# A mixture-of-experts stage: the inner features made turned, for three slots of tokens at once

## The chip, the cores and the metric

The program runs on one core of a Trainium2 chip. The metric is the device time of one execution in microseconds (us); lower is better. The kernel before takes 1195.88 us (median of three runs, 1195.74 to 1195.96).

The engines are named as in the profile: PE is TensorE (matrix multiply), PEld its weight loads, DVE is VectorE, ACT is ScalarE, POOL is GpSimd, SP is SyncE. Each works through its own queue in order.

## The reference

One block of a graph transformer on 1250 nodes with 768 features: a layer norm, a two-layer graph attention and a linear attention added to the input, and then a feed-forward layer with eight experts. The change concerns that last part alone:

```python
def _L0_ffn_ref(x, Wg, bg, W1, b1, W2, b2):      # DIM 768, 8 experts, HIDDEN 384, TOP_K 2
    gate = xt @ Wg + bg
    scores, idx = jax.lax.top_k(gate, TOP_K)
    h = jax.nn.gelu(jnp.einsum('td,edh->eth', xt, W1) + b1[:, None, :], approximate=False)
    y = jnp.einsum('eth,ehd->etd', h, W2) + b2[:, None, :]
    comb = jnp.sum(jax.nn.one_hot(idx, NUM_EXPERTS, dtype=x.dtype) * scores[..., None], axis=1)
    out = jnp.einsum('te,etd->td', comb, y)
...
x = x + _L0_ffn_ref(_layernorm(x, axis=-1)[None], ...)[0]
```

Every node goes to its two best experts, weighted with the raw scores. All is in float32.

## The kernel before

The program first builds the graph attention (up to line 581), then the linear attention (to 648), then, tile by tile of 125 nodes, queries, the sum of the branches, the second layer norm and the routing (lines 767 to 895). The normalised rows are written to a table in DRAM, `xl_d`; the sum so far goes to the output in DRAM. Routing leaves, for each expert, lists of node numbers in *slots* of 128 (`idx`) with the weights (`gs`).

The stage of the experts stands in lines 898 to 971. `slot` (line 904) computes one slot of 128 tokens for one expert:

1. an indirect DMA on POOL's queue gathers 128 rows of `xl_d` into `xg` (three buffers, line 908);
2. TensorE turns them in six transposes into `px` (two PSUM banks, one buffer, line 911), and two DVE copies bring them to `xsT` (line 915);
3. first layer: six matmuls with the tokens standing and 384 weight columns moving give `ph`, tokens on the partitions (line 919); DVE copies it to `h` (922), three more transposes turn it into `pt` (925), and three activations on ACT add the bias, now one number per partition, and apply the Gelu, into `hT` (928);
4. second layer: six matmuls with hT standing give `py` (two banks, one buffer, line 933);
5. DVE adds the bias (936), ACT multiplies by the gate weight (937) into `ys` (two buffers), and an indirect DMA on POOL's queue adds the 128 rows to the output in DRAM (938).

Each expert gets three slots in any case (`FIX`, lines 941 to 946). One further slot, of an expert that is only known at run time, is computed after that (`other(0)`, line 970), and more of them stand behind branches that are not taken here: the trace has 25 slots. Weights of an expert (2.3 MB, `expert`, line 653) lie in a ring of four buffers; the load for expert e + 4 is issued on SP's queue after expert e, and it needs the buffer that expert e's last matmul releases. The bias rows of the second layer have two buffers.

The order of instructions on each engine isn't the order of the text. A planner takes, by its own costs, the earliest instruction of the text that is ready when an engine is free; the engines then work through the order that results. Waits between engines, also the wait for a buffer and the wait of one scatter-add to the output for the one before it, are added automatically.

Of the kernel before, what the change touches and what calls it, by code (L numbers as in the profile page):

```python
# [27 lines left out]
F32 = mybir.dt.float32  # L28
# [5 lines left out]
AF = mybir.ActivationFunctionType  # L34
ALU = mybir.AluOpType
AX = mybir.AxisListType
PSUM = bass.MemoryType.PSUM

N, D = 1250, 768
PT, NT = 125, 10  # L40
KC = D // 128
H1, C1, H2, C2 = 4, 192, 2, 96
HEADS, DH = 12, 64
NE, FF = 8, 384
FC = FF // 128
# [8 lines left out]
NJ = -(-N // 128)  # L54
FIX = 3
# [14 lines left out]
def gps_block(ctx: ExitStack, tc: tile.TileContext, x, src, dst, norm_g, norm_b, W1, a_src1, a_dst1,  # L70
              b1, W2, a_src2, a_dst2, b2, Wu, bu, Wq, bq, Wk, bk, Wv, bv, Wo, bo, Wg, bg, fW1, fb1,
              fW2, fb2, out):
    nc = tc.nc
# [43 lines left out]
    ident = const.tile([128, 128], F32)  # L117
# [13 lines left out]
    xl_d = dram.tile([N + 128, D], F32)  # L131
# [40 lines left out]
    rows = fl.tile([KC, 128], F32)  # L172
# [67 lines left out]
    with tc.If(nc.values_load(odd[0:1, 0:1], min_val=0, max_val=1) > 0), ExitStack() as es:  # L240
# [9 lines left out]
        for j in range(NT):  # L250
# [21 lines left out]
            for g0 in range(0, NT, 4):  # L272
                n = min(4, NT - g0)
# [266 lines left out]
    with tc.tile_pool(name="wp", bufs=3) as wp, tc.tile_pool(name="rb", bufs=1) as rb:  # L540
        with tc.tile_pool(name="ag_p1", bufs=1, space=PSUM) as ag_p:
            for hd in range(H1):
# [10 lines left out]
                v = ag[:, :, :2 * CG].rearrange("p a (b c) -> p a b c", b=2)  # L553
# [44 lines left out]
    for t in range(NT):  # L598
# [3 lines left out]
        for k in range(2):  # L602
            half = slice(k * 384, (k + 1) * 384)
            for w in (Wk_sb, Wv_sb):
                ps = bank()
                for c in range(KC):
                    nc.tensor.matmul(ps[:PT, :384], xnT[:, c, t * PT:(t + 1) * PT], w[:, c, half],  # L607
                                     start=c == 0, stop=c == KC - 1)
# [11 lines left out]
            for c in range(3):  # L620
                nc.tensor.matmul(ps[:, c * 129:(c + 1) * 129],
                                 ky[:, (3 * k + c) * 128:(3 * k + c + 1) * 128], va[:, 3 * k + c],
                                 start=c == 0, stop=c == 2, skip_group_check=True)
# [29 lines left out]
    def expert(w1, w2, b2):  # L653

        t = wt.tile([128, KC, D], F32, name="w", bufs=4).rearrange("p c f -> p (c f)")
        nc.sync.dma_start(t[:, :KC * FF].rearrange("p (c f) -> p c f", c=KC),
                          w1.rearrange("(c p) f -> p c f", p=128))
        nc.sync.dma_start(t[:, KC * FF:].rearrange("p (c d) -> p c d", c=FC),
                          w2.rearrange("(c p) d -> p c d", p=128))
        b = fp.tile([128, D], F32, name="wb", bufs=2)  # L660
        nc.sync.dma_start(b, row_bcast(b2, 128))
        return t, b
# [27 lines left out]
    ring = [expert(fW1[0], fW2[0], fb2[0])]  # L690
    outr = out[:N].rearrange("(t p) d -> p t d", p=PT)
    xlr = xl_d[:N].rearrange("(t p) d -> p t d", p=PT)
    idx = fp.tile([128, NV + 1], I32)
    gs = fp.tile([128, NV + 1], F32)
    fb1T = fp.tile([128, FC, NE], F32)
# [3 lines left out]
    with ExitStack() as rs:  # L699
# [68 lines left out]
        for t in range(NT):  # L768
# [10 lines left out]
            for i, (l, r) in enumerate(parts):  # L779
                for k in range(2):  # L780
                    nc.tensor.matmul(po[k][:, :384], l, r[:, k * 384:(k + 1) * 384],  # L781
                                     start=i == 0, stop=i == len(parts) - 1)
# [5 lines left out]
            for h in range(H2):  # L788
                for k in range(2):
# [3 lines left out]
                                     stop=True)  # L793
# [9 lines left out]
            xT = rl.tile([128, KC, PT], F32, name="xT")  # L803
            turn(xT, xl, u_p, "u", nc.scalar.copy)
            pg = g_p.tile([128, 2 * NV], F32, name="g")
            for c in range(KC):
                nc.tensor.matmul(pg[:PT, :NE], xT[:, c], Wg_sb[:, c], start=c == 0,
                                 stop=c == KC - 1)
# [38 lines left out]
            for k in range(2):  # L847
# [3 lines left out]
                for i, v in enumerate((node1[:, t:t + 1], both[:, 1, k:k + 1])):  # L851
# [4 lines left out]
                                 stop=k == 1 and t == NT - 1)  # L856
# [9 lines left out]
        pt = g_p.tile([128, 2 * NV], F32, name="g")  # L866
# [32 lines left out]
    sp = ctx.enter_context(tc.tile_pool(name="sp", bufs=2))  # L899
    x_p = ctx.enter_context(tc.tile_pool(name="x_p", bufs=1, space=PSUM))  # L900
    h_p = ctx.enter_context(tc.tile_pool(name="h_p", bufs=2, space=PSUM))
    y_p = ctx.enter_context(tc.tile_pool(name="y_p", bufs=1, space=PSUM))

    def slot(w, rows, gates, bias):

        w, wb = w
        xg = sp.tile([128, D], F32, name="xg", bufs=3)
        nc.gpsimd.indirect_dma_start(xg, None, xl_d, bass.IndirectOffsetOnAxis(rows, 0))
        px = x_p.tile([128, 2, 512], F32, name="px")
        for c in range(KC):  # L910
            nc.tensor.transpose(px[:, c // 3, (c % 3) * 128:(c % 3 + 1) * 128],  # L911
                                xg[:, c * 128:(c + 1) * 128], ident)
        xT = sp.tile([128, KC, 128], F32, name="xsT")
        for a in range(2):
            nc.vector.tensor_copy(xT[:, 3 * a:3 * a + 3],  # L915
                                  px[:, a, :384].rearrange("p (b n) -> p b n", b=3))
        ph = h_p.tile([128, FF], F32, name="ph")
        for c in range(KC):
            nc.tensor.matmul(ph, xT[:, c], w[:, c * FF:(c + 1) * FF], start=c == 0,  # L919
                             stop=c == KC - 1)  # L920
        h = sp.tile([128, FF], F32, name="h")
        nc.vector.tensor_copy(h, ph)
        pt = h_p.tile([128, FC, 128], F32, name="pt")
        for f in range(FC):
            nc.tensor.transpose(pt[:, f], h[:, f * 128:(f + 1) * 128], ident)
        hT = sp.tile([128, FC, 128], F32, name="hT")
        for f in range(FC):
            nc.scalar.activation(hT[:, f], pt[:, f], AF.Gelu, bias=bias[:, f])  # L928
        py = y_p.tile([128, 2, 512], F32, name="py")
        for f in range(FC):  # L930
            for k in range(2):
                o = KC * FF + f * D + k * 384
                nc.tensor.matmul(py[:, k, :384], hT[:, f], w[:, o:o + 384], start=f == 0,  # L933
                                 stop=f == FC - 1)
        ys = sp.tile([128, D], F32, name="ys")
        nc.vector.tensor_add(halves(ys), py[:, :, :384], halves(wb))  # L936
        nc.scalar.mul(ys, ys, gates)
        nc.gpsimd.indirect_dma_start(out, bass.IndirectOffsetOnAxis(rows, 0), ys, None,
                                     compute_op=ALU.add)

    for e in range(NE):
        for j in range(FIX):
            v = e * NJ + j
            slot(ring[e], idx[:, v:v + 1], gs[:, v:v + 1], fb1T[:, :, e:e + 1])
        if e + 4 < NE:
            ring.append(expert(fW1[e + 4], fW2[e + 4], fb2[e + 4]))

    def other(k):

        ve = nc.values_load(v_row[0:1, k:k + 1], min_val=0, max_val=NV,  # L950
                            engines=[mybir.EngineType.DVE])
        ee = nc.values_load(e_row[0:1, k:k + 1], min_val=0, max_val=NE - 1,
                            engines=[mybir.EngineType.DVE, mybir.EngineType.SP])
        rows = sp.tile([128, 1], I32, name="rows")
        nc.vector.tensor_copy(rows, idx[:, bass.ds(ve, 1)])
        gates = sp.tile([128, 1], F32, name="gates")
        nc.vector.tensor_copy(gates, gs[:, bass.ds(ve, 1)])
        bias = sp.tile([128, FC, 1], F32, name="bias")
        nc.vector.tensor_copy(bias, fb1T[:, :, bass.ds(ee, 1)])
        w = expert(fW1[bass.ds(ee, 1)].rearrange("o d f -> (o d) f"),  # L960
                   fW2[bass.ds(ee, 1)].rearrange("o d f -> (o d) f"), fb2[bass.ds(ee, 1)])
        slot(w, rows, gates, bias)

    def others(k):
        if k < MORE:
            with tc.If(nc.values_load(n_more[0:1, 0:1], min_val=0, max_val=MORE) > k):
                other(k)
                others(k + 1)

    other(0)  # L970
    others(1)

# [31 lines left out]
```

## Time and profile before

| | |
|---|---|
| median of three runs | 1195.88 us |
| the profiled execution | 1195.09 us |
| its span, first to last instruction | 1193.0 us |
| graph and linear attention, 0 to 610 us | PE busy 543.69 |
| queries and routing, 610 to 936 us | PE busy 314.82 |
| experts, 936 to 1181.2 us | PE busy 234.81 of 245.20 |
| from the last scatter-add's issue to the end | 11.8 us |

"Busy" is the time in which at least one instruction of the engine ran. A float32 matmul stands in the trace as two records, so a matmul written once in the text counts twice. PEclk is the share of TensorE's full clock that was granted. A row of a group gives busy time and mean duration in ns, then the idle time of the engine just before, and what ended it. The mean duration of a PE record includes its way through the array; how far two records stand apart is read from their starts.

### The profile page before, as it was taken

How to read it: one execution, taken by the hardware profiler on the slowest of the kernel's cores; microseconds unless marked ns; L12 is line 12 of the kernel's file. 1: busy time of each engine (PE TensorE's matmuls, PEld its weight loads, DVE VectorE, ACT ScalarE, POOL GpSimd, SP SyncE). 2: the span in 40 equal slices, each digit the busy share in tenths (PEclk: the TensorE clock that was granted, in tenths of full speed). 3: DMA queues.
4: the chain of work that ended last, by engine and by line, in shares of the span. 5: the costliest groups of instructions: out<-in, count | busy, mean ns of one | idle time of the engine just before them, and what ended most of it. 6: DMA issues, size and time to landing. Idle time of an engine off the chain costs nothing.

```text
span 1193.0 us, 12366 instructions
## 1 busy us (share of the span) xinstructions
PE 1093.3 (92%) x4634; PEld 729.2 (61%) x4634; DVE 683.0 (57%) x1391; ACT 365.2 (31%) x575; POOL 76.8 (6%) x100
## 2 busy tenths in 40 slices
PE   2599988999999999899989999999998699999994
PEld 1586656587878788545545666666665455555552
DVE  6866666779797876696723655555555322222221
ACT  2141115273827272455621211111110012121121
POOL 1000000000000000000000000000000122232221
PEclk9599999999999999999989999999999699999998
DMA  5014000000000001000090111111134357667432
GB/s 154 27 50 162 20 20 1 1 1 1 1 1 1 1 1 53 1 0 1 29 385 4 39 39 39 39 39 39 39 118 158 118 143 195 178 175 184 104 67 42
DMA packets 33282, 79.62 MB, mean 67 GB/s; under 512 B 5258, under 2 KB 13020, under 8 KB 33208
## 3 DMA queue, kind: packets, MB, share of 16 engines
q1 hardware_dynamic: 27608, 59.02, 15.0%
q0 software_dynamic: 5600, 19.66, 8.2%
q8 instruction: 40, 0.66, 0.2%
q14 instruction: 34, 0.28, 0.1%
HBM read 60.37 MB, written 18.30 MB: 66 GB/s over the span
## 4 chain that ended last, share of the span: by engine, by line
PE 70%; DVE 21%; DMA 4%; issue 2%; ACT 2%; POOL 1%; DVEq 0%; SPq 0%; POOLq 0%; ACTq 0%
PE po L781 13%; PE ph L919 9%; PE py L933 7%; PE mm L430 7%; PE mm L607 7%; PE mm L751 7%; DVE scr L515 6%; DVE w L535 5%; DVE w L536 5%; PE ag L548 3%; PE u L792 2%; PE ag L569 2%; PE mm L405 2%; DMA w<-in_L_gnn_Wu_dram 2%; PE px L911 1%
## 5 line engine op out<-in xcount | busy, mean ns | idle before, releaser
L548 PE MATMUL ag<-kept,w 125*125 125x198 f32 x800 | 137.4, 333 | 5.1 <-DVE w L536 4.9
L548 PEld LDWEIGHTS ag<-kept,w 125*125 125x125 f32 x800 | 133.5, 188 | 9.0 <-DVE w L536 9.0
L919 PE MATMUL ph<-w,xsT 128*128 128x384 f32 x300 | 110.1, 505 | 3.2 <-DVE xsT L915 0.7
L933 PE MATMUL py<-w,hT 128*128 128x384 f32 x300 | 101.0, 487 | 0.5 <-ACT hT L928 0.5
L430 PE MATMUL mm<-Wg,xnT 128*125 128x400 f32 x240 | 91.0, 517 | 1.0 <-DVE xnT L321 0.6
L607 PE MATMUL mm<-Wv_sb,xnT 128*125 128x384 f32 x240 | 85.7, 489 | 4.8 <-DVE kvacc L627 4.8
L535 DVE TENSOR_TENSOR w<-v,w 125x1250 f32<-125x1250 f32 x60 | 86.3, 1454 | 5.9 <-ACT w L533 5.2
L936 DVE TENSOR_TENSOR ys<-py,wb 128x768 f32<-128x768 f32 x25 | 23.9, 957 | 113.9 <-issue 98.3
L781 PE MATMUL po<-w,xnT 128*125 128x384 f32 x240 | 84.8, 496 | 3.1 <-DMA w<-in_L_gnn_Wu_dram 3.1
L515 DVE CUSTOM_DVE_ANT_0 scr<-ss_row,mask 125x1250 bf16<-125x1250 f32 x60 | 87.2, 1453 | 0.5 <-ACT ss_row L506 0.2
L536 DVE SCALAR_TENSOR_TENSOR w<-w,AT 125x1250 f32<-125x1250 f32 x60 | 86.4, 1455 | 0.4
L534 ACT ACTIVATE v<-dn_row,sl 125x1250 f32<-125x1250 f32 x60 | 79.3, 1333 | 17.3 <-DVE w L535 16.8
L607 PE MATMUL mm<-Wk_sb,xnT 128*125 128x384 f32 x240 | 84.4, 486 | 0.0
L751 PE MATMUL mm<-w,xnT 128*125 128x384 f32 x240 | 84.2, 489 | 0.0
L919 PEld LDWEIGHTS ph<-w,xsT 128*128 128x128 f32 x300 | 56.3, 194 | 43.8 <-DVE xsT L915 9.0
L933 PEld LDWEIGHTS py<-w,hT 128*128 128x128 f32 x300 | 56.8, 190 | 40.4 <-ACT hT L928 1.2
L781 PE MATMUL po<-w,qT 128*125 128x384 f32 x240 | 80.8, 486 | 0.0
L781 PEld LDWEIGHTS po<-w,xnT 128*125 128x125 f32 x240 | 44.2, 190 | 30.6 <-DMA w<-in_L_gnn_Wu_dram 3.3
L781 PEld LDWEIGHTS po<-w,qT 128*125 128x125 f32 x240 | 44.2, 188 | 29.4
L607 PEld LDWEIGHTS mm<-Wv_sb,xnT 128*125 128x125 f32 x240 | 42.4, 187 | 31.1 <-DVE kvacc L627 6.9
L751 PEld LDWEIGHTS mm<-w,xnT 128*125 128x125 f32 x240 | 43.6, 188 | 27.6 <-ACT qT L321 0.2
L430 PEld LDWEIGHTS mm<-Wg,xnT 128*125 128x125 f32 x240 | 43.2, 192 | 26.8 <-ACT v L367 1.4
(277 smaller groups left out, 1436.3 us busy)
## 6 DMA issues: line engine op xcount, KB each, us to landing
w<-in_L_ffn_W_dram SPq DMA_DIRECT2D x18, 1152.0 KB
xt<-in_x_dram SPq DMA_DIRECT2D x20, 336.0 KB
wb<-in_L_ffn_b_dram SPq DMA_DIRECT2D x9, 384.0 KB
out_dram<-xt SPq DMA_DIRECT2D x10, 336.0 KB
xl_d<-xl SPq DMA_DIRECT2D x10, 336.0 KB
W_sb<-in_L_gnn_W_dram SPq DMA_DIRECT2D x1, 2304.0 KB
Wk_sb<-in_L_mix_Wk_dram SPq DMA_DIRECT2D x1, 2304.0 KB
Wv_sb<-in_L_mix_Wv_dram SPq DMA_DIRECT2D x1, 2304.0 KB
```

The lines of the kernel that those rows point to most:

```text
L430: nc.tensor.matmul(ps[:PT, :2 * (CG + 2)], xnT[:, c, t * PT:(t + 1) * PT], Wg1[:, c, 2 * k:2 * k + 2].rearrange("p h c -> p (h c)"), start ...
L515: nc.vector.tensor_tensor_reduce(scr, ss_row, mask[:, t], 1.0, 0.0, ALU.mult, ALU.max, top[:, t:t + 1])
L534: nc.scalar.activation(v, dn_row, AF.Exp, bias=sl[:, st:st + 1])
L535: nc.vector.tensor_tensor(w, v, w, op=ALU.max)
L536: nc.vector.scalar_tensor_tensor(w, w, 2.0, AT[:, st, :N], op0=ALU.min, op1=ALU.mult)
L548: nc.tensor.matmul(ag[:, t // 2, o:o + CG], w[:, t * PT:(t + 1) * PT], gw[:, st, hd], start=st == 0 and t % 2 == 0, stop=st == NT - 1, ski ...
L607: nc.tensor.matmul(ps[:PT, :384], xnT[:, c, t * PT:(t + 1) * PT], w[:, c, half], start=c == 0, stop=c == KC - 1)
L751: nc.tensor.matmul(ps[:PT, :384], xnT[:, c, tk], Wq_sb[:, c, half], start=c == 0, stop=c == KC - 1)
L781: nc.tensor.matmul(po[k][:, :384], l, r[:, k * 384:(k + 1) * 384], start=i == 0, stop=i == len(parts) - 1)
L919: nc.tensor.matmul(ph, xT[:, c], w[:, c * FF:(c + 1) * FF], start=c == 0, stop=c == KC - 1)
L933: nc.tensor.matmul(py[:, k, :384], hT[:, f], w[:, o:o + 384], start=f == 0, stop=f == FC - 1)
L936: nc.vector.tensor_add(halves(ys), py[:, :, :384], halves(wb))
```

## The change

`slot` is split in three. `gather(rows)` fetches and turns the rows of up to three slots into one `xsT` of 384 columns. `hidden` makes the inner features already turned: the weights' 128 x 128 blocks stand, and the tokens' columns, 384 of them, move, so that the bias and Gelu go straight from `ph` to `hT`; the copy to `h` and the transposes to `pt` go. `give` is the second layer and the scatter-add for one slot, as before. The loop over experts calls `hidden` for an expert, then `gather` for the next one, then `give` three times. `py` gets two buffers, in the banks that `pt` leaves. The slot known only at run time goes through the same functions with one slot of 128 columns.

```diff
-    y_p = ctx.enter_context(tc.tile_pool(name="y_p", bufs=1, space=PSUM))
-
-    def slot(w, rows, gates, bias):
+    y_p = ctx.enter_context(tc.tile_pool(name="y_p", bufs=2, space=PSUM))
+
+    def gather(rows):
+
+        xT = sp.tile([128, KC, FIX * 128], F32, name="xsT")
+        for j, r in enumerate(rows):
+            xg = sp.tile([128, D], F32, name="xg", bufs=3)
+            nc.gpsimd.indirect_dma_start(xg, None, xl_d, bass.IndirectOffsetOnAxis(r, 0))
+            px = x_p.tile([128, 2, 512], F32, name="px")
+            for c in range(KC):
+                nc.tensor.transpose(px[:, c // 3, (c % 3) * 128:(c % 3 + 1) * 128],
+                                    xg[:, c * 128:(c + 1) * 128], ident)
+            for a in range(2):
+                nc.vector.tensor_copy(xT[:, 3 * a:3 * a + 3, j * 128:(j + 1) * 128],
+                                      px[:, a, :384].rearrange("p (b n) -> p b n", b=3))
+        return xT
+
+    def hidden(w, xT, n, bias):
+
+        hT = sp.tile([128, FC, FIX * 128], F32, name="hT")
+        for f in range(FC):
+            ph = h_p.tile([128, 512], F32, name="ph")
+            for c in range(KC):
+                o = c * FF + f * 128
+                nc.tensor.matmul(ph[:, :n * 128], w[0][:, o:o + 128], xT[:, c, :n * 128],
+                                 start=c == 0, stop=c == KC - 1)
+            nc.scalar.activation(hT[:, f, :n * 128], ph[:, :n * 128], AF.Gelu, bias=bias[:, f])
+        return hT
+
+    def give(w, hT, j, rows, gates):
 
         w, wb = w
...
-        ph = h_p.tile([128, FF], F32, name="ph")
-        for c in range(KC):
-            nc.tensor.matmul(ph, xT[:, c], w[:, c * FF:(c + 1) * FF], start=c == 0,
-                             stop=c == KC - 1)
-        h = sp.tile([128, FF], F32, name="h")
-        nc.vector.tensor_copy(h, ph)
-        pt = h_p.tile([128, FC, 128], F32, name="pt")
-        for f in range(FC):
-            nc.tensor.transpose(pt[:, f], h[:, f * 128:(f + 1) * 128], ident)
-        hT = sp.tile([128, FC, 128], F32, name="hT")
-        for f in range(FC):
-            nc.scalar.activation(hT[:, f], pt[:, f], AF.Gelu, bias=bias[:, f])
         py = y_p.tile([128, 2, 512], F32, name="py")
         for f in range(FC):
             for k in range(2):
                 o = KC * FF + f * D + k * 384
-                nc.tensor.matmul(py[:, k, :384], hT[:, f], w[:, o:o + 384], start=f == 0,
-                                 stop=f == FC - 1)
+                nc.tensor.matmul(py[:, k, :384], hT[:, f, j * 128:(j + 1) * 128], w[:, o:o + 384],
+                                 start=f == 0, stop=f == FC - 1)
...
+    def fixed(e):
+        return [(idx[:, v:v + 1], gs[:, v:v + 1]) for v in range(e * NJ, e * NJ + FIX)]
+
+    xT = gather([r for r, _ in fixed(0)])
     for e in range(NE):
-        for j in range(FIX):
-            v = e * NJ + j
-            slot(ring[e], idx[:, v:v + 1], gs[:, v:v + 1], fb1T[:, :, e:e + 1])
+        hT = hidden(ring[e], xT, FIX, fb1T[:, :, e:e + 1])
+        if e + 1 < NE:
+            xT = gather([r for r, _ in fixed(e + 1)])
+        for j, (rows, gates) in enumerate(fixed(e)):
+            give(ring[e], hT, j, rows, gates)
         if e + 4 < NE:
             ring.append(expert(fW1[e + 4], fW2[e + 4], fb2[e + 4]))
...
-        slot(w, rows, gates, bias)
+        hT = hidden(w, gather([rows]), 1, bias)
+        give(w, hT, 0, rows, gates)
```

More of the change, by code (lines that the diff above doesn't have):

```diff
@@ L901, in gps_block @@
     h_p = ctx.enter_context(tc.tile_pool(name="h_p", bufs=2, space=PSUM))
-    y_p = ctx.enter_context(tc.tile_pool(name="y_p", bufs=1, space=PSUM))
-    def slot(w, rows, gates, bias):
-        w, wb = w
-        xg = sp.tile([128, D], F32, name="xg", bufs=3)
-        nc.gpsimd.indirect_dma_start(xg, None, xl_d, bass.IndirectOffsetOnAxis(rows, 0))
-        px = x_p.tile([128, 2, 512], F32, name="px")
-        for c in range(KC):
[L911 to L916, printed above, removed]
-        ph = h_p.tile([128, FF], F32, name="ph")
-        for c in range(KC):
-            nc.tensor.matmul(ph, xT[:, c], w[:, c * FF:(c + 1) * FF], start=c == 0,
-                             stop=c == KC - 1)
-        h = sp.tile([128, FF], F32, name="h")
-        nc.vector.tensor_copy(h, ph)
-        pt = h_p.tile([128, FC, 128], F32, name="pt")
-        for f in range(FC):
-            nc.tensor.transpose(pt[:, f], h[:, f * 128:(f + 1) * 128], ident)
-        hT = sp.tile([128, FC, 128], F32, name="hT")
-        for f in range(FC):
-            nc.scalar.activation(hT[:, f], pt[:, f], AF.Gelu, bias=bias[:, f])
```

## The prediction

> **What bounds the kernel now.** I read four views: the page, the waits from 880 us on, the instructions in order of time, and the table of stretches. The page first: the share of TensorE in the chain that ended last, and where the expert stage (lines 904 to 962) stands in it.
>
> ```profile
> span 1193.0 us, 12366 instructions
> PE 70%; DVE 21%; DMA 4%; issue 2%; ACT 2%; POOL 1%; DVEq 0%; SPq 0%; POOLq 0%; ACTq 0%
> PE po L781 13%; PE ph L919 9%; PE py L933 7%; PE mm L430 7%; PE mm L607 7%; PE mm L751 7%; DVE scr L515 6%; DVE w L535 5%; DVE w L536 5%; PE ag L548 3%; PE u L792 2%; PE ag L569 2%; PE mm L405 2%; DMA w<-in_L_gnn_Wu_dram 2%; PE px L911 1%
> L919 PE MATMUL ph<-w,xsT 128*128 128x384 f32 x300 | 110.1, 505 | 3.2 <-DVE xsT L915 0.7
> L933 PE MATMUL py<-w,hT 128*128 128x384 f32 x300 | 101.0, 487 | 0.5 <-ACT hT L928 0.5
> ```
>
> The stage from 936.5 us on is TensorE's. A float matmul is two records ("passes"): 300 for 25 slots x 6. The stretches (columns: length, then busy time of PE, PEld, DVE, ACT, POOL; clock; DMA share; GB/s) and one slot in order of time:
>
> ```profile
> 940.00:950.00 10.00, 8.92 (x24) 5.44 (x24) 1.46 (x3) 0.00 (x0) 1.11 (x2) 0.59 0.39 117
> 979.68:1007.62 27.94, 27.62 (x101) 16.52 (x100) 7.61 (x12) 5.46 (x12) 7.73 (x6) 1.00 0.70 183
> ```
>
> ```profile
> 1023.15 1.59 POOL L938 DMA_INDIRECT out_dram<-ys,idx  x1 [4.67 <-ACT ys L937]
> ...
> 1023.92 0.82 PE L911 MATMUL px<-ident,xg 128*128 128x128 f32 x6
> ...
> 1024.12 0.56 DVE L922 COPY h<-ph 128x384 f32<-128x384 f32 x1 [2.21 <-PE ph L919]
> ...
> 1024.73 0.55 PE L925 MATMUL pt<-ident,h 128*128 128x128 f32 x3
> 1024.77 1.02 DVE L915 COPY xsT<-px 128x384 f32<-128x384 f32 x2
> ...
> 1025.38 0.91 PE L919 MATMUL ph<-w,xsT 128*128 128x384 f32 x2
> ...
> 1026.13 4.03 PE L933 MATMUL py<-w,hT 128*128 128x384 f32 x12
> ...
> 1030.00 3.39 PE L919 MATMUL ph<-w,xsT 128*128 128x384 f32 x10
> ```
>
> Three slots are one expert: 27.94 us, TensorE busy all of it at full clock. The starts give the budget of a slot (1023.92 to 1033.23, 9.31 us): 12 py passes take 1030.00 - 1026.13 = 3.87, so 0.3225 a pass, and 24 take 7.74; 9 transposes take 0.109 each (six px are 0.67 in the chain), 0.98; the rest, 0.6, is waiting: pt for the copy of h (0.16), ph for the copies of xsT (0.33), py for the Gelu (0.1). The order on TensorE is: a piece that is ready and stands later in the program fills a hole (px and ph of the next slot before pt of this one). I use that below.
>
> **The change, part by part.**
>
> *Hidden layer turned.* Before: 6 matmuls a slot, tokens standing, 384 weight columns moving. After: 18 an expert, weights standing, 384 token columns moving. 36 passes an expert either way, same shapes, same price: nothing. Removed: three pt transposes a slot (9 x 0.109 = 0.98 an expert), the copy of h (0.56 of DVE), and the three waits above (1.8 an expert). Gelu becomes 3 of 384 columns instead of 9 of 128 (366 ns each); ScalarE is busy 5.5 of 27.94, so this is hidden under the passes. The second layer begins with the first third of hT, whose Gelu ran two thirds of a layer ago; the last third is needed 8 passes (2.6 us) later. No wait.
>
> *Expert in steady state.* 72 x 0.3225 + 18 x 0.109 = 25.18. New waits: px has one buffer, so the second and third slots' transposes each wait for two DVE copies (1.02 + some 0.2 of signals). Since second-layer passes are ready, they should fill the hole, as px does now; a hole judged too short costs what it costs now, 0.16 to 0.33. Bounds: 0 and 2 x 1.2; I take 0.25 each, 0.5 an expert, by the nearest row (pt and ph above). So 25.7 against 27.94.
>
> *First expert.* Its first layer now needs three gathers. They are issued at 936.46, 937.94, 939.21, as before; the first lands at 940.4 and the others follow their issues, so DMA isn't the limit, px is: transposes 1.55 at half clock, copies 1.02, 0.1 of signals, about 2.7 a slot. 940.43 + 2 x 2.7 + 1.55 + 0.6 = 948.0 for the first pass, against 942.62: +5.4. The next expert's three gathers cost POOL 3 x 0.99 and hide behind that layer.
> The Trainium skill, "TensorE: Matmul & The Clock Gate" (Part 1), speaks against this: after about 3.4 us with little matmul work the clock is halved until one full window of that length was busy. The row above agrees (clock 0.59; the first 12 passes took 6.91 instead of 3.87, 2.9 lost). By the row I would charge the same 2.9 again; by the rule the windows are fixed in time, clock rose near 948.2, so the next edge is 951.6: 3.6 us at half rate, 1.8 lost. If 948.2 is missed by a little it is one window more, +1.7. I take 1.8; the row's value would make the sum 1.1 longer.
>
> *Scatter-adds come in bursts.* The gives of one expert follow each other at 3.87 us, not 9.31. A scatter-add waits for the one before to land:
>
> ```profile
> POOL out_dram L938 <- DMA out_dram<-ys,idx: 37.8, 5, 8.2
> DMA to landing us min/median/max: 5.5/5.7/10.3
> ```
>
> (the second line is of the scatters; the waits' columns are total, times, longest). "DMA: Bandwidth & Descriptors" (Rules for kernel authors) asks for that wait between accumulating DMAs, and its fixed-plus-size price (Anatomy of one DMA) would make 393 KB about 2.9 us; the trace says 5.7, and about 10 beside an expert's weights. I use the trace: 5.95 a link with the next issue. An expert's three links: 5.95 + 5.95 + one that lands with the weights (11.4 to 12.3 us after these start, five times) come to some 25.2 in 25.7. It just fits; by the page's price it would fit with 12 to spare. Behind a waiting scatter on POOL stand the next gathers. A gather waits only for px of the slot whose buffer it takes, and those transposes come before the gives, so all three leave POOL some 3 us before the first scatter of the expert is ready, and have over 15 us to land (5.4 median, 9.8 longest). A late scatter delays the third ys add of an expert (two ys buffers). Behind that add stand, on DVE, the px copies of the next expert (some 12 us later), on ScalarE its own scaling and the next Gelu (3.9 us later), and its py bank pair, wanted again by the second give of the next expert, 16 us on. All covered as long as the first scatter lands within about 3 us of the last give.
> On SP the next weights are released by the last give, as now, and have three experts' time: nothing.
>
> *Last slot.* 36 passes of 128 columns instead of 12 of 384. The nearest row is the 129-column matmul of L621, six in 0.91 to 0.94 including 0.28 of depth, so 0.11 to 0.13: 4.0 to 4.7 against 3.87. I take 4.0. Its px and copies are no longer covered: 0.65 + 1.3.
>
> *The sum on the profiled execution.* First pass 948.0; 576 passes 185.8 and 1.8 cold; 7 x 18 transposes 13.7; waits 3.5: last give ends 1152.8. Last slot 0.65 + 1.3 + 4.0 + 3.87 = 9.8: 1162.6. From the last pass to the last scatter 2.56 as now (1178.67 to 1181.23): 1165.1; the scatter chain from expert 7's first give (1145.0 + 2.56 + 3 x 5.95) gives 1165.4. From there to the end 11.8 as now. Span 1177.2, 15.8 below 1193.0. That execution lasted 1195.09, 0.8 below the median of the runs, 1195.88; taking 15.8 off the median: 1180.
>
> **The rivals.**
>
> *Tail burst.* The last slot's first layer is slipped in before expert 7's gives. Then only one give follows and the chain of four scatters ends about 5 us after TensorE: 1185. For it: the present order fills holes from later slots. Against: the new order should have no hole there.
>
> *Transposes in a block.* The three px of an expert stand next to each other and TensorE waits out both copies: 2 x 1.2 x 7 = 17 in place of 3.5: 1194, no change. Against: second-layer passes are ready at that time.
>
> *Slower: the gather behind the scatters.* If the third gather for the expert after next stands behind the third scatter on POOL, then while weights load: last give, weights landed 13.4 later, scatter 1.9, gather landed 5.4, transposes 0.65, two and a half gives 10: 31.3 an expert, five times, +28: 1208. It decides when that gather leaves POOL later than some 33 us after its expert's predecessor began its first layer. For it: one queue, in order, and the waits above. Against: the gather is ready first.
>
> *Scatter chain as bound.* If two links an expert, not one, run at 10 or more: about 29 an expert in five, 1197.
>
> *Better.* No wait left at px and the last px filled in earlier: 1174.
>
> That it does nothing (the removed work was hidden) is excluded: the stretch has no idle TensorE to hide nine transposes in.
>
> **How the numbers follow.** Likeliest 0.66 (1175 to 1187), tail burst 0.10, block 0.10, gather behind 0.08, chain 0.03, better 0.03. A change under 0.2% (2.4 us) can't be told from none. The block, at 1194, is split 0.05 faster, 0.03 same, 0.02 slower. Faster: 0.66 + 0.10 + 0.03 + 0.05 = 0.84; same 0.03; slower: 0.08 + 0.03 + 0.02 = 0.13. The range 1173 to 1194 takes in better, tail and most of block and leaves out 0.11 to 0.15.
>
> **What would show it.** Right: rows for pt and h gone; ph still 0.32 a pass; an expert's stretch near 25.7; first pass of ph near 948; three gathers in a row on POOL, before three scatters that each wait for a DMA. Wrong: TensorE idle before px for "DVE xsT" or for "DMA xg", ys waiting for a scatter with py behind it, or a clock under 1.00 after 955 us.

## The result, and the profile after

The changed kernel takes 1179.32 us (median of five runs, 1178.16 to 1181.04); the kernel before took 1195.74 us beside it (1191.18 to 1195.96). The ratio is 0.9874, with a 95% interval of 0.9852 to 0.9895. The forecast was 1180 us, 1173 to 1194. Where an experiment below gives no ratio, its time is that of a single execution.

From the page of the changed kernel: the span, the chain that ended last by line, and the groups of the two layers.

```profile
span 1178.6 us, 12106 instructions
PE po L781 13%; PE ph L926 8%; PE py L938 7%; PE mm L430 7%; PE mm L607 7%; PE mm L751 7%; DVE scr L515 6%; DVE w L535 5%; DVE w L536 5%; PE ag L548 3%; PE ag L569 2%; PE u L792 2%; PE px L912 2%; PE mm L405 2%; DMA w<-in_L_gnn_Wu_dram 2%
L926 PE MATMUL ph<-xsT,w 128*128 128x384 f32 (+1 forms) x324 | 100.6, 470 | 1.8 <-DVE xsT L915 1.8
L938 PE MATMUL py<-w,hT 128*128 128x384 f32 x300 | 100.6, 486 | 0.0
```

The rows of pt and h are gone. The 324 passes of ph are 8 x 36 with 384 columns and 36 with 128 for the last slot. TensorE still leads the chain, and before py it never stood idle.

The stretches of the changed kernel: the first 20 us of the experts' stage and one expert in steady state (columns as in the prediction).

```profile
940.00:950.00 10.00, 5.41 (x20) 3.99 (x21) 3.24 (x7) 0.00 (x0) 3.77 (x4) 0.50 0.60 185
950.00:960.00 10.00, 10.00 (x28) 5.70 (x27) 0.00 (x0) 2.44 (x3) 0.00 (x0) 0.83 0.14 39
976.60:1001.92 25.32, 25.32 (x92) 15.35 (x91) 5.94 (x9) 4.54 (x6) 7.69 (x6) 1.00 0.76 202
```

An expert takes 25.32 us where it took 27.94. The first ten microseconds, with 5.41 of TensorE's time at a clock of 0.50, are the price of turning three slots' rows before the first pass: their transposes and copies take turns, as px has one buffer.

The order in the changed kernel, one expert in time:

```profile
988.21 0.82 PE L912 MATMUL px<-ident,xg 128*128 128x128 f32 x6
...
988.87 1.46 PE L938 MATMUL py<-w,hT 128*128 128x384 f32 x4
989.07 1.02 DVE L915 COPY xsT<-px 128x384 f32<-128x384 f32 x2 [10.85 <-PE px L912]
989.16 1.55 POOL L943 DMA_INDIRECT out_dram<-ys,idx  x1 [9.66 <-ACT hT L928]
...
990.19 0.85 PE L912 MATMUL px<-ident,xg 128*128 128x128 f32 x6
...
991.01 1.02 POOL L909 DMA_INDIRECT xg<-xl_d,idx  x1 [0.30 <-issue]
```

The copies of px run while four passes of py do: four passes are 1.29 us, the copies 1.02 and their signals, and the next px starts 1.32 us after these passes did.

The end, from the chain in order of time of the changed kernel (start, length, what):

```profile
1140.24 3.88 PE py L938 x12
...
1146.41 5.65 DMA out_dram<-ys,idx
...
1152.81 6.41 DMA out_dram<-ys,idx
...
1159.97 5.95 DMA out_dram<-ys,idx
...
1166.68 1.54 POOL out_dram L943
```

After expert 7's first give, no more matmul stands in the chain: four scatter-adds do, the last three each waiting for the one before. The last pass of TensorE starts at 1161.33; the last scatter-add starts 5.34 us later, where it was 2.78.

The other stages hold the same work but drift from one execution to the next: in this one the first gather is issued at 937.47, before it was 936.46. So below I also give *the stage*: from the start of the first gather to the start of the last scatter-add, in the profiled execution. Before it is 244.8 us, after 229.2.

### The profile page after: what moved, and what is told of

Its sections match the earlier page's. It is cut to its first block, busy times and chain, and to the rows that moved or that the text cites. A ratio compares the mean times of both kernels' runs of the same rounds, so it can differ in the third digit from the quotient of the medians.

```text
span 1178.6 us, 12106 instructions
## 1 busy us (share of the span) xinstructions
PE 1077.8 (91%) x4583; PEld 723.6 (61%) x4583; DVE 669.1 (57%) x1366; ACT 358.1 (30%) x527; POOL 76.3 (6%) x100
## 4 chain that ended last, share of the span: by engine, by line
PE 70%; DVE 20%; DMA 5%; issue 2%; ACT 2%; POOL 1%; DVEq 0%; SPq 0%; POOLq 0%; ACTq 0%
PE po L781 13%; PE ph L926 8%; PE py L938 7%; PE mm L430 7%; PE mm L607 7%; PE mm L751 7%; DVE scr L515 6%; DVE w L535 5%; DVE w L536 5%; PE ag L548 3%; PE ag L569 2%; PE u L792 2%; PE px L912 2%; PE mm L405 2%; DMA w<-in_L_gnn_Wu_dram 2%
## 5 line engine op out<-in xcount | busy, mean ns | idle before, releaser
L926 PE MATMUL ph<-xsT,w 128*128 128x384 f32 (+1 forms) x324 | 100.6, 470 | 1.8 <-DVE xsT L915 1.8
L926 PEld LDWEIGHTS ph<-xsT,w 128*128 128x128 f32 x324 | 59.8, 193 | 41.4 <-DVE xsT L915 2.4
L915 DVE COPY xsT<-px 128x384 f32<-128x384 f32 x50 | 25.5, 552 | 99.2 <-PE px L912 77.3
L751 PEld LDWEIGHTS mm<-w,xnT 128*125 128x125 f32 x240 | 43.6, 188 | 27.6 <-ACT qT L321 0.2
```

The costliest lines, as they stand in the source:

```text
L751: nc.tensor.matmul(ps[:PT, :384], xnT[:, c, tk], Wq_sb[:, c, half], start=c == 0, stop=c == KC - 1)
L915: nc.vector.tensor_copy(xT[:, 3 * a:3 * a + 3, j * 128:(j + 1) * 128], px[:, a, :384].rearrange("p (b n) -> p b n", b=3))
L926: nc.tensor.matmul(ph[:, :n * 128], w[0][:, o:o + 128], xT[:, c, :n * 128], start=c == 0, stop=c == KC - 1)
```

## The experiments

The theory: TensorE sets the time of the stage, so it falls by the transposes taken out and the waits around them. The rivals: three slots of columns at once are what pays; or the look ahead to the next rows; or the second py; and scatter-adds or copies bind somewhere.

**e1: turned, but one slot at a time, in the order of before.**

```diff
-    xT = gather([r for r, _ in fixed(0)])
     for e in range(NE):
-        hT = hidden(ring[e], xT, FIX, fb1T[:, :, e:e + 1])
-        if e + 1 < NE:
-            xT = gather([r for r, _ in fixed(e + 1)])
-        for j, (rows, gates) in enumerate(fixed(e)):
-            give(ring[e], hT, j, rows, gates)
+        for rows, gates in fixed(e):
+            hT = hidden(ring[e], gather([rows]), 1, fb1T[:, :, e:e + 1])
+            give(ring[e], hT, 0, rows, gates)
```

> The inner features stay turned, but one slot of 128 tokens moves at a time (36 passes of 128 columns), and the order of the text is again slot after slot. If the gain is the removed transposes and waits, three slots at once bring nothing: a pass of 128 columns is about 0.11 us (the last slot of the changed kernel took 36 in 4.0), a slot 4.0 + 3.87 + 0.65 = 8.5 us, 25 slots 213 to 215; the first layer starts 5.5 us earlier and the scatter-adds, 8.5 us apart, no longer queue at the end (2.3): about 1174, below the changed kernel. If three slots at once are what pays, because a short pass waits for its weights (0.19 each), a slot is 11.4 us and the kernel takes about 1250.

Measured: 1203.62 us, ratio to before 1.0064 (1.0047 to 1.0080); the stage is 253.4. Slower than before, which neither theory had. One slot of it in order of time:

```profile
1013.16 0.82 PE L912 MATMUL px<-ident,xg 128*128 128x128 f32 x6
...
1013.42 0.96 DVE L941 TENSOR_TENSOR ys<-py,wb 128x768 f32<-128x768 f32 x1 [7.84 <-issue]
...
1014.29 1.01 DVE L915 COPY xsT<-px 128x384 f32<-128x384 f32 x2
...
1014.89 4.29 PE L926 MATMUL ph<-xsT,w 128*128 128x128 f32 x36 [0.91 <-DVE xsT L915]
...
1019.01 4.04 PE L938 MATMUL py<-w,hT 128*128 128x384 f32 x12
```

The short passes cost what I expected, 1014.89 to 1019.01 for 36 (0.114 each), so weights don't limit them. But px now stands bare in front of its own first layer: transposes 0.65, then the add of ys, which DVE has in front of the copies, then the copies, and TensorE waits 0.91 in every slot. Before, the hole in which pt waited for h had been filled with the next slot's px. With pt gone, no px was moved ahead; that this is for want of a hole is argued from the two orders, not shown. A slot is 9.73 us against 9.31: the transposes are 0.33 less, the waits 0.5 more, and the short passes 0.25 more than 12 of 384 columns.

**e2: every transpose of px twice.**

```diff
-            for c in range(KC):
+            for c in [*range(KC), *range(KC)]:
```

> The changed kernel with each of the six transposes of a slot's rows made twice, to the same place. If TensorE bounds the stage without a hole, each of 25 slots gets 0.65 us longer: +16, about 1195.5. If TensorE waits for copies, rows or scatters anyway, the extra transposes vanish in the waits: +3 or less.

Measured: 1194.74 us. An expert in this kernel:

```profile
1019.36:1046.64 27.28, 27.28 (x110) 17.33 (x109) 5.94 (x9) 4.54 (x6) 7.71 (x6) 1.00 0.74 192
```

It takes 1.96 us more than the changed kernel's 25.32, which is 18 x 0.109. In steady state TensorE has no room left, and what is added to it lengthens an expert in full. The stage grows a little less than 25 slots' worth, by 14.1 us (243.3 against 229.2). One reason is at the end, where the last scatter-add starts 3.6 us after the last pass does, not 5.3.

**e3: one buffer of py.**

```diff
-    y_p = ctx.enter_context(tc.tile_pool(name="y_p", bufs=2, space=PSUM))
+    y_p = ctx.enter_context(tc.tile_pool(name="y_p", bufs=1, space=PSUM))
```

> The changed kernel with one buffer of py, as before. If the gain is the removed transposes and waits, the second buffer is worth little: four passes of the next first layer stand between two gives and cover most of the 1.2 us until the add has read py: 0 to +3 us. If the second buffer is what pays, each of 17 gives that follow another of their expert waits 1.2 us: +20, about 1199.

Measured: 1179.15 us, the stage 229.9. From the order on TensorE:

```profile
1017.57 1.45 PE L926 MATMUL ph<-xsT,w 128*128 128x384 f32 x4
1018.86 4.12 PE L938 MATMUL py<-w,hT 128*128 128x384 f32 x12
1022.81 1.45 PE L926 MATMUL ph<-xsT,w 128*128 128x384 f32 x4
1024.10 4.12 PE L938 MATMUL py<-w,hT 128*128 128x384 f32 x12
```

Four passes of the next first layer fill the hole, and the second py buffer is worth some 0.7 us of the stage.

**e4: the next expert's rows turned after the gives.**

```diff
-        if e + 1 < NE:
-            xT = gather([r for r, _ in fixed(e + 1)])
         for j, (rows, gates) in enumerate(fixed(e)):
             give(ring[e], hT, j, rows, gates)
+        if e + 1 < NE:
+            xT = gather([r for r, _ in fixed(e + 1)])
```

> The changed kernel with the next expert's rows turned after the gives. If the placement of the gather between the layers matters as worked out, the three groups of transposes stand in a block, TensorE waits for two pairs of copies (1.2 each) and for the first of the last pair (0.6) in seven experts: +21, about 1200, which is more than the change brings. If the copies are hidden anyway: 1179.

Measured: 1216.81 us, the stage 267.2: 38 us above the changed kernel, not 21. The stretches of the block of px and of the first layer behind it, in this kernel:

```profile
1002.04:1008.78 6.74, 3.17 (x19) 2.35 (x17) 3.52 (x7) 0.94 (x1) 2.58 (x2) 0.79 0.68 214
1008.78:1022.47 13.69, 13.69 (x37) 7.90 (x38) 0.41 (x1) 1.16 (x2) 3.57 (x3) 0.85 0.86 240
```

and the same time cut where the clock changed:

```profile
1002.55:1005.96 3.41, 1.15 (x9) 0.70 (x7) 2.35 (x4) 0.94 (x1) 2.37 (x2) 1.00 0.75 233
1005.96:1009.37 3.41, 2.10 (x7) 1.64 (x8) 1.58 (x4) 0.00 (x0) 0.22 (x1) 0.50 0.78 243
1009.37:1012.79 3.42, 3.42 (x7) 1.69 (x6) 0.00 (x0) 0.00 (x0) 0.00 (x0) 0.50 1.05 287
```

The block takes 6.74 us where its transposes are 1.96 and the expectation made 5.0 of it: an add of ys stands in front of the copies here too, and the clock fell inside the block. It was 0.5 from 1006.0 to 1012.8, and the 36 passes took 13.7 instead of 11.6. The clock fell in five of the seven blocks, for 3.4 us in four of them and 6.8 in this one. So of the 17 us beyond the expectation, about 8 are in the blocks and 9 in the first layers behind them.

The Trainium skill's page "TensorE: Matmul & The Clock Gate" (Part 1), used in the prediction for the start alone, halves the clock after an idle window of about 3.4 us. That length agrees with these stretches. The condition does not: no hole was longer than 2.0 us, and TensorE was busy 1.15 to 1.61 us of the 3.41 before each fall. With three slots at once, the look ahead is worth more than the whole change.

**e5: one slot at a time, with the next slot's rows between the layers.**

```diff
+    line = [(e, r, g) for e in range(NE) for r, g in fixed(e)]
+    xT = gather([line[0][1]])
+    for i, (e, rows, gates) in enumerate(line):
+        hT = hidden(ring[e], xT, 1, fb1T[:, :, e:e + 1])
+        if i + 1 < len(line):
+            xT = gather([line[i + 1][1]])
+        give(ring[e], hT, 0, rows, gates)
...
```

> One slot of 128 tokens at a time as in e1, but the next slot's rows are turned between the two layers of this one. In e1 a slot took 9.73 us: 0.65 + 4.0 + 3.87 and 1.1 of waiting for the copies of px, which stood bare in front of their own first layer. If that bare wait is what made e1 slow, it goes under the second layer: a slot 8.5 to 8.6, and from the first gather to the last scatter-add some 227 us, where the changed kernel has 229.2 and before 244.8: about 1177. If 128-column passes or the 25 first layers of 128 tokens are the loss in e1, it stays near 1200.

Measured: 1175.22 us, ratio 0.9842 (0.9811 to 0.9873), the stage 225.8. Against e1 the text differs in one place, where the next rows are asked for, and the stage is 27.6 us shorter. A slot:

```profile
1007.96 0.82 PE L912 MATMUL px<-ident,xg 128*128 128x128 f32 x6
...
1008.61 4.04 PE L938 MATMUL py<-w,hT 128*128 128x384 f32 x12
1008.81 1.02 DVE L915 COPY xsT<-px 128x384 f32<-128x384 f32 x2 [3.66 <-PE px L912]
...
1012.48 4.18 PE L926 MATMUL ph<-xsT,w 128*128 128x128 f32 x36
```

Three slots are 25.63 us; three at once are 25.32. So three slots' columns at once are worth 0.3 us an expert; they put the first pass 5.3 us later (1.3 of it are two slots' transposes, which only change places with the first layer) and cost 2.6 at the end. By the stage, one slot at a time with the look ahead is 3.4 us shorter than the changed kernel; the intervals of the two ratios overlap.

**e6: the first and last expert one slot at a time, the six between three at once, and the last slot's rows before the last give.**

```diff
+    line = [(e, part) for e in range(NE)
+            for part in ([[s] for s in fixed(e)] if e in (0, NE - 1) else [fixed(e)])]
+    xT = gather([r for r, _ in line[0][1]])
+    for i, (e, part) in enumerate(line):
+        hT = hidden(ring[e], xT, len(part), fb1T[:, :, e:e + 1])
+        if i + 1 < len(line):
+            xT = gather([r for r, _ in line[i + 1][1]])
+        else:
+            late = first_other()
+        for j, (rows, gates) in enumerate(part):
+            give(ring[e], hT, j, rows, gates)
...
```

> The changed kernel with the first and the last expert's slots one at a time (turned, next rows between the layers), the six experts between three at once, and the last slot's rows turned before the last give. If the costs of three at once are its later start (first layer 11.7 us after the first gather, 6.2 before) and the burst of scatter-adds at the end (last scatter 5.3 us after the last second-layer pass starts, 2.8 before), both go: -5.4, -2.5, -1.3 for the bare px of the last slot, +0.8 for short passes: some 221 us from the first gather to the last scatter-add, about 1171. If the end is set by the scatter chain in any case, only the start is won: 1175.

Measured: 1172.86 us, ratio 0.9812 (0.9782 to 0.9841), the stage 223.3. The start (first layer 6.2 us after the first gather) and the end (2.8) are as expected; between them TensorE took 214.3 us where I had worked out 211.7. The trace places those 2.6: 1.3 are the transposes of the first expert's second and third slot, which now stand behind the first pass; about 0.7 more is lost at the half clock, which rose at 949.0, 6.0 us after the first pass (4.2 in the changed kernel); and 0.6 is in two first layers of the last expert (4.40 and 4.23 us instead of 4.02), whose cause stays open.

**e7: every second slot added to a table of its own.**

```diff
...
-        nc.gpsimd.indirect_dma_start(out, bass.IndirectOffsetOnAxis(rows, 0), ys, None,
-                                     compute_op=ALU.add)
+        sinks[0] += 1
+        nc.gpsimd.indirect_dma_start(alt if sinks[0] % 2 else out,
+                                     bass.IndirectOffsetOnAxis(rows, 0), ys, None,
+                                     compute_op=ALU.add)
```

> The changed kernel with every second slot added to a table of its own in DRAM, so that a scatter-add waits for the one two before it (the output lacks the slots of the other table). If the queue of scatter-adds costs time at the end alone, the last one is issued 2.8 us after the last second-layer pass starts, not 5.3: -2.5, and an expert stays at 25.3 us. If it also slows the experts, they come down too: -8 or more.

Measured: 1177.32 us, the stage 226.3. The end in this kernel:

```profile
1156.85 4.04 PE L941 MATMUL py<-w,hT 128*128 128x384 f32 x12
...
1160.98 0.96 DVE L944 TENSOR_TENSOR ys<-py,wb 128x768 f32<-128x768 f32 x1 [7.84 <-PE py L941]
1161.97 0.93 ACT L945 ACTIVATE ys<-ys,gates 128x768 f32<-128x768 f32 x1 [4.55 <-DVE ys L944]
1163.18 1.55 POOL L947 DMA_INDIRECT alt<-ys,rows  x1 [8.17 <-ACTq L983]
```

The last scatter-add follows the last pass as it did before, 2.78 us after its start, and an expert stays at 25.3. The queue of scatter-adds costs 2.6 us, at the end alone.

**e8: three slots and the look ahead, but the first layer not turned (with one py, as in e3).**

```diff
-        for f in range(FC):
-            ph = h_p.tile([128, 512], F32, name="ph")
...
+        for j in range(n):
+            at = slice(j * 128, (j + 1) * 128)
+            ph = h_p.tile([128, FF], F32, name="ph")
+            for c in range(KC):
+                nc.tensor.matmul(ph, xT[:, c, at], w[0][:, c * FF:(c + 1) * FF], start=c == 0,
+                                 stop=c == KC - 1)
+            h = sp.tile([128, FF], F32, name="h")
+            nc.vector.tensor_copy(h, ph)
+            pt = h_p.tile([128, FC, 128], F32, name="pt")
+            for f in range(FC):
+                nc.tensor.transpose(pt[:, f], h[:, f * 128:(f + 1) * 128], ident)
+            for f in range(FC):
+                nc.scalar.activation(hT[:, f, at], pt[:, f], AF.Gelu, bias=bias[:, f])
```

> Three slots at once and the next rows between the layers, one py, but the first layer as before: tokens standing, then the copy to h and three transposes a slot. Against e3 (one py, turned; 229.9 us from the first gather to the last scatter-add). If the turned features are what pays, the nine transposes come back at 0.98 an expert and up to 1 us of waiting: 238 to 246 us, 1187 to 1195. If looking ahead is what pays and the transposes hide, 230 to 232 us.

Measured: 1183.00 us, the stage 234.8, between the two expectations. An expert in this kernel, what its transposes still wait for, and a part of the order on TensorE:

```profile
1010.86:1037.40 26.54, 26.54 (x102) 16.12 (x101) 7.62 (x13) 5.45 (x12) 7.72 (x6) 1.00 0.75 193
```

```profile
PE pt L932 <- DVE h L929: 0.7, 1, 0.7
```

```profile
1027.05 2.74 PE L926 MATMUL ph<-w,xsT 128*128 128x384 f32 x8
1029.63 0.49 PE L932 MATMUL pt<-ident,h 128*128 128x128 f32 x3
1029.96 4.04 PE L926 MATMUL ph<-w,xsT 128*128 128x384 f32 x12
1033.83 0.49 PE L932 MATMUL pt<-ident,h 128*128 128x128 f32 x3
1034.16 2.75 PE L926 MATMUL ph<-w,xsT 128*128 128x384 f32 x8
1036.74 0.82 PE L912 MATMUL px<-ident,xg 128*128 128x128 f32 x6
1037.40 0.81 PE L944 MATMUL py<-w,hT 128*128 128x384 f32 x2
```

The nine transposes cost 26.54 - 25.48 (an expert of e3) = 1.06 us an expert, hardly more than their own 0.98, and wait once in the whole stage. The other 1.4 us of an expert (27.94 to 26.54) go though the transposes stay: first-layer passes of another slot cover the copy to h, and second-layer passes cover the copies of px.

**e9 and e10: the changed kernel and e6 side by side.** No new edit.

> The changed kernel itself, on the same chip and in the same rounds as e10, so that the two can be compared: 0.987 of the kernel before, as at first.

> The kernel of e6 again beside the changed one. From the first gather to the last scatter-add e6 took 223.3 us, the changed kernel 229.2: if that is the difference of the kernels and not of the day, e10 stays 5 to 7 us below e9, at about 0.982 of the kernel before; if the other stages' drift made it, they are equal within 2 us.

Measured: 1179.22 us, ratio 0.9872 (0.9857 to 0.9887), the stage 229.3, for the changed kernel; 1173.40 us, ratio 0.9826 (0.9813 to 0.9840), the stage 222.7, for e6's. The mixed kernel is 5.8 us faster than the changed one. Its median is the lowest of all that were run; against e5 the stage is 2.5 to 3.1 us shorter, but the intervals of the ratios overlap.

## Why the prediction was right

The sum, term by term, each from the first gather on:

| | predicted | measured |
|---|---|---|
| first pass of ph | 11.5 | 11.66 |
| that to the end of expert 7's gives | 204.8 | 202.6 |
| last slot to its last pass's end | 9.8 | 10.0 |
| to the last scatter-add | 2.8 | 5.0 |
| the stage | 228.9 | 229.2 |

Two terms were off and cancelled, so it is luck that the sum came within 0.3 us. The mechanism, TensorE without a hole in steady state, was right.

*New waits at px.* I took 0.25 us each, by the nearest row; an expert of 25.32 against 25.18 of pure work leaves 0.14 for two. The planner left four passes, 1.29 us, for copies and signals that need about 1.2. With the cold start a little dearer (36 passes in 13.93 instead of 11.61, so 2.3, not 1.8), the second row comes out 2.2 us short.

*The burst at the end.* The mechanism was named, and that the last slot's first layer would stand behind expert 7's gives was right: the tail rival's order did not come. But I let the chain of scatter-adds end 0.3 us after TensorE's work, with 5.95 a link. The links were 6.40, 7.16 and 6.70: landings of 5.65 to 6.41, and 0.75 from a landing to the next start. e7 shows that term alone: 2.6 us. By the price that the prediction takes from the Trainium skill's "DMA: Bandwidth & Descriptors" (Anatomy of one DMA), an estimate of 2.9 us, a link of 2.9 + 0.75 would be shorter than the 3.87 between two gives, and there would have been no such term; the landings here decide against it.

*What takes the waits away.* This step was wrong, though the sum was not. I booked the three waits of a slot (1.8 an expert) to the turned layer. e8 keeps the transposes and loses 1.4 of the 1.8; e1 has the turned layer and a new wait of 0.9 in each slot. It is the new order of the text that removes the waits, and the turning that removes 1.0 us of transposes an expert. Of the stage's 15.6 us, 9.9 are there without turning (244.77 to 234.83, e8). Turning adds 5.0 (e8 to e3), net of a start that is 5.3 us later and an end that is 2.4 later; the second py brings the rest. e8 has three slots at once and the look ahead together. No run has one of them alone with an unturned first layer, so how the 9.9 divide between them is not shown.

*The rivals.* The block of transposes, which I priced at no change (1194), is dearer than that: e4, 1216.8, as I left out the add of ys in front of the copies on DVE, and the clock. The gathers did stand behind a waiting scatter-add on POOL: at 989.16 the third one of the expert before is issued, late, and the three gathers follow from 991.01. They are wanted some 22 us later; the point from which the slower rival decides was not reached. The scatter chain never bound an expert (e7). Half of one of my signs of being wrong did occur: the add of ys waited for a scatter-add to land, eight times and 26.5 us in all. But TensorE never waited for py behind it.

## What to carry to other kernels

When a planner fills holes, the order of the text is part of the tuning: work that was hidden in a hole stands bare when the hole is removed. With the transposes of h taken out and the order left as it was, this kernel became slower (e1); asking for the next rows one step earlier in the text took 27.6 us off the stage (e5). And batching costs at both ends, a later start and a burst of dependent stores. Here it gains only 0.3 us an expert, and it pays when it is kept for the middle of the loop, with small steps at the ends (e6, e10).

## What the runs showed of the hardware

A float32 pass of 128 columns takes 0.114 us in a run of 36 (e1), with a weight load of its own before each pass, though the row of such a load says 0.19; a pass of 384 columns takes 0.3225. So narrow columns cost little here: a slot's first layer takes 4.12 us (e1) or 4.02 (e5) against 3.87.

The clock was halved behind holes of at most 2.0 us (e4). TensorE had been busy 1.15 to 1.61 us of the 3.41 before each of the five falls. No threshold follows: three other such stretches with 1.59, 1.66 and 1.69 us were followed by no fall.

The clock rose behind a stretch of transposes (e2, at the start of the stage):

```profile
949.71:953.12 3.41, 2.76 (x13) 2.36 (x13) 0.64 (x2) 0.00 (x0) 0.41 (x1) 0.50 0.42 115
953.12:956.53 3.41, 3.41 (x11) 2.09 (x12) 0.38 (x1) 0.00 (x0) 0.54 (x1) 1.00 0.40 115
```

The first matmul of the first layer starts at 953.09, so all of the 2.76 us but 0.03 are transposes, and the clock was at full from 953.12. The first layer then took 11.7 us, where it takes 13.9 in the changed kernel.
